# Row maxima turned by VectorE, DMAs and ScalarE instead of a TensorE transpose, for five of eight row tiles

## The chip, the cores and the metric

The kernel runs on one core of a Trainium2 chip. The metric is the device time of one execution, in microseconds; of the kernel before, three runs gave a median of 757.19 us (756.47 to 757.96). All arithmetic is 32-bit floating point.

## The reference

For each of 8 samples of 1024 rows by 256 columns an adaptive layer norm, an attention and a feed-forward stage follow each other. Cut to what matters:

```python
h = _layernorm(x) * (1 + ca) + sa
scores = einsum('nsd,ntd->nst', h * w_lhs, h * w_rhs)
x = x + ga * einsum('nst,ntd->nsd', softmax(scores, axis=2), h)
h = _layernorm(x) * (1 + cb) + sb
x = x + gb * (relu(h @ W1 + b1) @ W2 + b2)
```

The softmax takes the maximum of each row of scores away before the exponential. This maximum is what the change is about.

## The kernel before, in words

A sample b has 8 row tiles i of 128 rows. The scores are symmetric up to the two weight vectors that are folded in, so `direct` (L403) computes only the blocks on and right of the diagonal on TensorE; ScalarE copies them out of PSUM (L419), and `mirror` (L424) fills in the blocks left of it: VectorE turns 32x32 blocks (L435), four DMAs write them to a scratch tensor in DRAM (D_m, L306), and one DMA reads them back into the score tile sc (L309).

Three helpers then make the weights of a tile.

- `row_max` (L461): VectorE reduces the tile's 1024 scores to m, one maximum for each of 128 rows, one in each partition (L463).
- `max_turn` (L466): TensorE multiplies m, repeated along the columns, with the identity in transpose mode. The result pm in PSUM holds the 128 maxima along a row, the same row in every partition (L468).
- `subtract` (L471) and `exponent` (L483): VectorE subtracts pm from the eight blocks of scores into pT (L475), ScalarE takes the exponential in place (L484).

The products with pT run on TensorE as `product` (L493) or, for the pairs of tiles (1,2), (3,4) and (6,7) from the second sample on, in `pair_begin` and `pair_end` with seven products of halves in place of eight; GpSimd makes the sums of the halves (L565, L575 to L577).

The order of the work is written out by hand, in the loop over b and i that begins at L1150, and `pin` keeps every engine to it. Tile (b, i) is processed together with the scores of the tile two further on (`ahead`, L1153); its maxima are taken in the iteration before the one that turns them. In iteration i of sample b the feed-forward stage of sample b-1 (its second layer's sums, Y) runs in between:

- `pair_products` (L728) issues five or six feed-forward products for a block c and, between two of them, calls the function that it was handed, which is `max_turn` in iterations 0, 1 and 4. ScalarE's copy `kept` (L747) comes before that call.
- in iterations 2, 3, 6 and 7 `max_turn` is called inside `y_first`, `y_second` or `pair_begin`.
- the second sample is special at its start: in (1, 0) the maxima of two tiles are turned, those of (1,0) in the first `pair_products` and those of (1,1) in the second one (L1243), and only then comes the exponential of (1,0) (L1245).

The feed-forward stage's results go through DRAM as well to be turned: `turn_blocks` and `y_turn` (L316, L862) on VectorE, four DMAs out (D_a, D_f, D_y, L306), one back (X_a, X_f, Y, L309). All of these DMAs are issued by SyncE (SP) in one order; the read waits at SP for its four writes to land. X_a feeds ScalarE's rT and lT (L342), which the next sample's scores use; X_f feeds hT (L705, L707) and GpSimd's sums hs (L714 to L717), which `pair_products` uses; Y is added to x by GpSimd (L880).

PSUM is held in three pools: two buffers for scores, two for transposes and pm, and four (`ps_a`) for all other products, so a product waits until VectorE has read the one that had its buffer.

Of the kernel before, what the change touches and what calls it, by code (L numbers as in the profile page):

```python
# [11 lines left out]
F32 = mybir.dt.float32  # L12
# [5 lines left out]
P = 128  # L18
# [6 lines left out]
def adaln_block_kernel(  # L25
# [13 lines left out]
    nc = tc.nc  # L39
    B, S, D = x.shape  # L40
# [5 lines left out]
    TH = HALF // P  # L46
    H2 = HALF // 2
    NH = NI // 2
    V = 32
    NV = P // V  # L50
    DX = D + 4

    const = ctx.enter_context(tc.tile_pool(name="const", bufs=1))
    two = ctx.enter_context(tc.tile_pool(name="two", bufs=2))
    work = ctx.enter_context(tc.tile_pool(name="work", bufs=3))
# [38 lines left out]
    early_d = two.tile([P, 4, D], F32, tag="X", name="early_d", bufs=1)  # L94
# [7 lines left out]
    def load_x0(q, queue):  # L102
# [11 lines left out]
        out=wv[ND : 2 * ND, :], in_=w_rhs.rearrange("a b (k p) -> (a b k) p", p=P)  # L114
# [19 lines left out]
    ident = const.tile([P, P], F32, name="ident")  # L134
# [5 lines left out]
    def warm(n):  # L140
# [9 lines left out]
            name=nc.get_next_instruction_name(),  # L150
# [6 lines left out]
    NC_ = ND * B  # L157
# [1 line left out]
        nc.tensor.transpose(pt_c[:, ts(k, B)], c_sb[:, ts(k, P)], ident[:B, :B])  # L159
    scT = const.tile([P, ND, B], F32, name="scT")  # L160
    scf = scT.rearrange("p k b -> p (k b)")
    den = const.tile([P, NC_], F32, name="den")
    nc.scalar.activation(den, pt_c[:, :NC_], AF.Exp, scale=-1.0)

    def silu():
# [90 lines left out]
    def prepare_start(b):  # L256
        xg_t[b] = two.tile([P, NT, DX], F32, tag="xg", name=f"xg_{b}")
        nc.gpsimd.memset(xg_t[b][:, :, D : D + 1], 1.0)
# [134 lines left out]
    def score_row(b, i):  # L393
        if b == 0:
            return first_scores()[:, i].rearrange("p (n v) -> p n v", v=V)
        return sc_t[b].rearrange("p i a j v -> p j (i a) v")[:, i]
# [61 lines left out]

    max_t, pT_t = {}, {}

    def row_max(b, i):  # L461
        m = work.tile([P, 1], F32, tag="m", name=f"m_{b}_{i}")
        nc.vector.tensor_reduce(m, score_row(b, i), AX.XY, ALU.max)  # L463
        max_t[b, i] = m

    def max_turn(b, i):  # L466
        pm = ps_t.tile([P, HALF], F32, tag="t", name=f"pm_{b}_{i}")
        nc.tensor.transpose(pm[:, :P], max_t.pop((b, i)).to_broadcast([P, P]), ident)  # L468
        pT_t[b, i] = pm

    def subtract(b, i):  # L471
# [48 lines left out]


    XS = D - P + 1
    tsum = const.tile([P, 4, TH, P + 4], F32, name="tsum")
    nc.gpsimd.memset(tsum[:, 1, :, P : P + 1], 1.0)

    def right_sums(b, which):

        xg = xg_t[b]
        b11, b12 = xg[:, 0:TH, P:D], xg[:, 0:TH, 0:P]
        b21, b22 = xg[:, TH:NT, P:D], xg[:, TH:NT, 0:P]  # L530
        t = [tsum[:, n, :, 0:P] for n in range(4)]
        ins = [(b12, b11), (b22, t[0]), (b22, b12), (t[1], b21)]
        for n in which:
            nc.gpsimd.tensor_tensor(t[n], *ins[n], ALU.subtract)
# [44 lines left out]
    def pair_end(b, i):  # L579

        (s2, s4), (s3, a22) = halves(pT_t.pop((b, i))), halves(pT_t.pop((b, i + 1)))
        s1 = two_t.pop("s1")
        pq = ps_a.tile([P, HALF], F32, tag="a", name=f"pq_{b}_{i}")
        pr = ps_a.tile([P, HALF], F32, tag="a", name=f"pr_{b}_{i}")
        for out, lhs, rhs in (
            (pr[:, P : 2 * P], s1, tsum[:, 0, :, 0:P]),
            (pq[:, XS : XS + P], a22, tsum[:, 3, :, 0:P]),
            (pr[:, 2 * P : 3 * P], s3, tsum[:, 2, :, 0:P]),
            (pq[:, 0:XS], s2, tsum[:, 1, :, 0:XS]),
            (pr[:, 0:P], s4, xg_t[b][:, TH:NT, 0:P]),  # L590
        ):
            for t in range(TH):
                nc.tensor.matmul(  # L593
                    out, lhsT=lhs[:, t, :], rhs=rhs[:, t, :],
                    start=(t == 0), stop=(t == TH - 1),
                )
        two_t[b, i] = two_t[b, i][0], pq, pr
# [411 lines left out]
    def first_rows():  # L1009

        pr = ps_a.tile([P, HALF], F32, tag="a", name="prow")
        nc.tensor.matmul(
            pr[:, :HALF],
            lhsT=ident[:, 0:1].to_broadcast([P, P]),
            rhs=early_c[:, 0:2, :].rearrange("b j d -> b (j d)"),
            start=True,
            stop=True,
        )
        return pr
# [7 lines left out]
    def make_gcol():  # L1027
# [9 lines left out]
    pr = first_rows()  # L1037
# [6 lines left out]
        ALU.mult,  # L1044
    )
    row_max(0, 0)
    xg_half(0)
    mirror(0, 0)
    xg_half(1)
    keep_rows(pr, 1)  # L1050
    direct(0, 2)
    max_turn(0, 0)
    row_max(0, 1)
    for g in range(2):
        x_plus(0, g)
    subtract(0, 0)
    mirror(0, 1)
    exponent(0, 0)
    mod_rows(3, 2)
    max_turn(0, 1)  # L1060
    subtract(0, 1)
    while queue:
# [87 lines left out]
    for b in range(B):  # L1150
        for i in range(NT):
# [8 lines left out]
            if (b, i) == (0, NT - 2):  # L1160

                prepare_turn(1, 1)
                product(b, i)
                direct(*ahead)
                exponent(*last_exponent)
                product_out(b, i)
                mirror(*ahead)
                early(b, i)
                for _ in range(4):
                    spare()  # L1170
                norms(b, i)
                row_max(*ahead)
                late, last_exponent = ahead, None
                continue
            if ahead and ahead != (0, 2):
                direct(*ahead)
            if b == 0:
# [17 lines left out]
                if ahead[0] == 0:  # L1195
                    max_turn(*ahead)
# [8 lines left out]
                if i == NT - 1:  # L1205
                    assert not queue
                    right_sums(1, range(4))
# [80 lines left out]
            else:  # L1288
# [5 lines left out]
                if i == 2:  # L1294
                    left_sums(b, 1)
                elif i == 3:
                    pair_begin(b, i, turn_max)
                elif i == 6:
                    pair_begin(b, i, lambda: (max_turn(*late), weights(*late)))
                elif not ahead:  # L1300

                    pair_end(b, i - 1)
                    pair_out(b, i - 1)
                    pair_stats(b, i - 1)
# [48 lines left out]
            if i in (0, 5):  # L1353
                product(b, i)
                product_out(b, i)
            elif i == 1:
                pair_begin(b, i)
                pair_begin_sum(b, i)
            elif i == 3:
                left_sums(b, i)  # L1360
            elif i in (2, 4) or i == NT - 1 and ahead:
                pair_end(b, i - 1)
                pair_out(b, i - 1)
                if i == NT - 1:
                    assert not queue
                    right_sums(b + 1, range(4))
                if i == NT - 1 or b == B - 1:
                    pair_stats(b, i - 1)
# [8 lines left out]
    b = B - 1  # L1377
# [74 lines left out]
```

## Time and profile before

| What | Value |
|---|---|
| median of three runs | 757.19 us |
| the profiled execution's own time | 756.93 us |
| its span, first to last instruction | 755.1 us |
| PE idle, all waits of its matmuls together | 2.7 us |
| mean granted clock of TensorE | 1.000 |
| DMA packets, of these under 512 B | 106213, 29700 |
| exponentials, subtractions, maxima, turns of maxima | 64 each |

The profile is of one execution on the one core. PE is TensorE's matmul, PEld its weight load, DVE VectorE, ACT ScalarE, POOL GpSimd, SP SyncE; SPq marks a DMA issue by SP. Busy times of engines overlap. A line of the timeline gives the start, the length, the engine, the source line, the operation and its tiles, and in brackets how long the engine was idle before it and what ended that. A sample takes about 90.5 us, and from the third sample on the pattern repeats with that period.

### The profile page before, as it was taken

Reading aid. Unit: us, or ns where it says so; the run is one execution under the profiler, and the core shown is the slowest. Engines: PE = TensorE matmul, PEld = TensorE weight load, DVE = VectorE, ACT = ScalarE, POOL = GpSimd, SP = SyncE. Lnnn points to the kernel's source line nnn. Section 1 sums busy time; section 2 is a strip of 40 time slices with the busy share of each in tenths; the row PEclk is TensorE's granted clock in tenths of the full one; section 3 lists DMA queues with packets and bytes.
Section 4 is the critical chain, followed back from the end, with each engine's and each line's share of the span. In section 5 each row is a group of like instructions: output and inputs, shape, how many; then the busy total and the mean of one; then the engine's idle time right before and its main releaser. Section 6 shows DMA issues by size and latency. Waiting matters only on the chain.

```text
span 755.1 us, 11883 instructions
## 1 busy us (share of the span) xinstructions
PE 749.1 (99%) x3876; PEld 623.4 (83%) x3876; DVE 574.9 (76%) x1259; ACT 374.9 (50%) x688; POOL 570.9 (76%) x658
## 2 busy tenths in 40 slices
PE   8999999999999999999999999999999999999998
PEld 4686889788897888888888878988889788888887
DVE  7787879778796879968878688876889777685632
ACT  4554646635375454745546444563546535252521
POOL 3762796878968798788877699777996888669741
PEclk9999999999999999999999999999999999999999
DMA  9033442455443453445534555245553354133220
GB/s 308 16 112 98 131 133 74 135 178 152 127 120 123 153 153 110 147 118 158 164 99 119 153 154 161 74 127 172 155 152 85 119 166 133 50 91 126 84 85 28
DMA packets 106213, 95.21 MB, mean 126 GB/s; under 512 B 29700, under 2 KB 98848, under 8 KB 106152
## 3 DMA queue, kind: packets, MB, share of 16 engines
q1 hardware_dynamic: 98408, 85.81, 38.6%
q10 hardware_dynamic: 7744, 8.65, 3.7%
q8 instruction: 30, 0.49, 0.3%
q14 instruction: 31, 0.25, 0.1%
HBM read 50.62 MB, written 43.81 MB: 125 GB/s over the span
## 4 chain that ended last, share of the span: by engine, by line
PE 96%; DMA 1%; DVE 1%; ACT 1%; issue 0%
PE psc L412 16%; PE pa L726 11%; PE po L501 10%; PE pr L593 7%; PE pb L726 7%; PE pc L726 7%; PE yc L806 6%; PE ya L806 6%; PE yb L806 6%; PE pq L593 5%; PE pp L549 5%; PE py L916 4%; PE yd L806 3%; DMA wm<-in_L_wmod_dram 1%; PE pm L468 1%; PE pmr L194 0%
## 5 line engine op out<-in xcount | busy, mean ns | idle before, releaser
L412 PE MATMUL psc<-rT,lT 128*128 128x512 f32 (+3 forms) x384 | 134.8, 487 | 0.0
L780 POOL TENSOR_TENSOR f<-f,kept 128x512 f32<-128x512 f32 x64 | 81.5, 1274 | 42.8 <-DVE f L779 20.1
L419 ACT COPY sc<-psc 128x512 f32<-128x512 f32 (+3 forms) x96 | 44.7, 476 | 119.9 <-PE psc L412 113.0
L484 ACT ACTIVATE pT<-pT 128x1024 f32<-128x1024 f32 x64 | 67.6, 1056 | 70.6 <-DVE pT L475 70.5
L475 DVE TENSOR_TENSOR pT<-sc,pm 128x1024 f32<-128x1024 f32 x64 | 77.3, 1208 | 29.3 <-PE pm L468 13.7
L412 PEld LDWEIGHTS psc<-rT,lT 128*128 128x128 f32 x384 | 66.4, 191 | 37.2 <-issue 25.6
L501 PE MATMUL po<-xg,pT 128*128 128x257 f32 x352 | 80.6, 380 | 0.0
L463 DVE TENSOR_REDUCE m<-sc 128x1 f32<-128x1024 f32 x64 | 77.4, 1209 | 2.2 <-ACT sc L419 1.8
L501 PEld LDWEIGHTS po<-xg,pT 128*128 128x128 f32 x352 | 66.2, 190 | 10.0 <-issue 0.7
L747 ACT COPY kept<-pa 128x512 f32<-128x512 f32 x64 | 37.4, 584 | 69.3 <-PE pa L726 69.1
L726 PE MATMUL pb<-hs,w1s 128*128 128x256 f32 x256 | 65.9, 380 | 0.1
L726 PE MATMUL pc<-hT,w 128*128 128x256 f32 x256 | 65.7, 379 | 0.0
L880 POOL TENSOR_TENSOR x<-x,Y 128x512 f32<-128x512 f32 x28 | 35.1, 1276 | 29.3 <-DMA Y<-D_y 29.3
L789 ACT ACTIVATE f<-f 128x512 f32<-128x512 f32 x64 | 39.8, 622 | 34.7 <-POOL f L780 34.7
L642 POOL TENSOR_TENSOR x<-x,rows 128x256 f32<-128x256 f32 x64 | 44.8, 732 | 13.8 <-ACT rows L1022 10.6
L726 PEld LDWEIGHTS pb<-hs,w1s 128*128 128x128 f32 x256 | 48.5, 190 | 7.3 <-DVE f L765 0.8
L726 PEld LDWEIGHTS pc<-hT,w 128*128 128x128 f32 x256 | 48.6, 190 | 6.7
L806 PE MATMUL yc<-f,w2s 128*128 128x256 f32 x224 | 51.3, 379 | 0.0
L435 DVE STREAM_TRANSPOSE Tm<-sc 128x896 f32<-128x896 f32 (+6 forms) x49 | 34.3, 701 | 20.3 <-ACT sc L419 19.6
L806 PEld LDWEIGHTS yc<-f,w2s 128*128 128x128 f32 x224 | 41.5, 190 | 8.1 <-issue 2.9
L549 PEld LDWEIGHTS pp<-xg,pT 128*128 128x128 f32 x336 | 41.9, 192 | 5.1 <-DVE st_b L241 1.4
L799 POOL TENSOR_TENSOR ft<-f 128x256 f32<-128x256 f32 x56 | 40.8, 729 | 6.8 <-ACT f L790 6.8
(166 smaller groups left out, 1821.1 us busy)
## 6 DMA issues: line engine op xcount, KB each, us to landing
D_f<-T_f SPq DMA_DIRECT2D x60, 128.0 KB, 2.5
X_f<-D_f SPq DMA_DIRECT2D x15, 512.0 KB, 3.7
D_a<-T_a SPq DMA_DIRECT2D x56, 128.0 KB, 2.8
D_y<-T_y SPq DMA_DIRECT2D x56, 128.0 KB, 2.9
Y<-D_y SPq DMA_DIRECT2D x14, 512.0 KB, 3.4
out_dram<-x SPq DMA_DIRECT2D x14, 512.0 KB, 4.4
X_a<-D_a SPq DMA_DIRECT2D x13, 512.0 KB, 3.4
x<-in_L_attn_x_dram ACTq DMA_DIRECT2D x12, 512.0 KB, 3.4
```

Of the source, the lines that this page charges most:

```text
L412: nc.tensor.matmul(psc[:, : hi - lo], lhsT=lT_t[b, i // TH][:, k, ts(i % TH, P)], rhs=rT_t[b, n][:, k, lo - n * HALF : HALF], start=(k == ...
L419: nc.scalar.copy(score_row(b, i)[:, lo // V : hi // V, :], psc[:, : hi - lo].rearrange("p (n v) -> p n v", v=V),)
L463: nc.vector.tensor_reduce(m, score_row(b, i), AX.XY, ALU.max)
L475: nc.vector.tensor_tensor(pT.rearrange("p j (a v) -> p j a v", v=V), score_columns(b, i), pm[:, :P].rearrange("p (j a v) -> p j a v", j=1, ...
L484: nc.scalar.activation(pT_t[b, i], pT_t[b, i], AF.Exp)
L501: nc.tensor.matmul(po[:, : D + 1], lhsT=pT[:, t, :], rhs=xg_t[b][:, t, 0 : D + 1], start=(t == 0), stop=(t == NT - 1),)
L549: nc.tensor.matmul(out, lhsT=lhs[:, t, :], rhs=xg_t[b][:, h * TH + t, P : P + XS], start=(t == 0), stop=(t == TH - 1),)
L593: nc.tensor.matmul(out, lhsT=lhs[:, t, :], rhs=rhs[:, t, :], start=(t == 0), stop=(t == TH - 1),)
L642: queue.append(lambda: nc.gpsimd.tensor_tensor(out, in0, row, op))
L726: nc.tensor.matmul(out, lhsT=lhsT, rhs=rhs, start=True, stop=True)
L780: nc.gpsimd.tensor_tensor(f[:, c::NH, hi], f[:, c::NH, hi], kept[:, None, hi].to_broadcast([P, 2, H2]), ALU.add,)
L806: nc.tensor.matmul(out, lhsT=lhs(c), rhs=rhs(c), start=(c == 0), stop=(c == NH - 1))
```

## The change

For tiles 0, 1, 2, 4 and 5 of the samples b = 1 to 7, 35 tiles in all, `max_turn` no longer uses TensorE. `row_max` itself starts the work: VectorE turns 32x32 blocks of m, repeated to 32 columns, into mb, so that the partitions 0, 32, 64 and 96 each hold 32 of the maxima in a row; four DMAs on SP's queue, one for each of these partitions, copy its 128 bytes into all 128 partitions of mt, from SBUF to SBUF; and at the place where `max_turn` stood, ScalarE copies mt into the PSUM tile pm. The subtraction reads pm as before. The other 29 turns stay on TensorE.

mb and mt have one buffer each. To make room, the rows of xg lose two unused columns (DX), two small tiles change their layout (tsum) or move into a tile that has room (den). The other engines' orders do not change.

```diff
-    DX = D + 4
+    DX = D + 2
...
-    den = const.tile([P, NC_], F32, name="den")
+    den = early_d[:, 2, P : P + NC_]
...
+    in_time = lambda b, i: b > 0 and i in (0, 1, 2, 4, 5)
+
     def row_max(b, i):
         m = work.tile([P, 1], F32, tag="m", name=f"m_{b}_{i}")
         nc.vector.tensor_reduce(m, score_row(b, i), AX.XY, ALU.max)
         max_t[b, i] = m
+        if not in_time(b, i):
+            return
+
+        mb = work.tile([P, V], F32, tag="mb", name=f"mb_{b}_{i}", bufs=1)
+        nc.vector.transpose(mb, m.to_broadcast([P, V]))
+        mt = max_t[b, i] = work.tile([P, NV, V], F32, tag="mt", name=f"mt_{b}_{i}", bufs=1)
+        for a in range(NV):
+            nc.sync.dma_start(
+                out=mt[:, a],
+                in_=mb[a * V : a * V + 1].rearrange("o (n v) -> o n v", n=1).to_broadcast([1, P, V]),
+            )
 
     def max_turn(b, i):
         pm = ps_t.tile([P, HALF], F32, tag="t", name=f"pm_{b}_{i}")
-        nc.tensor.transpose(pm[:, :P], max_t.pop((b, i)).to_broadcast([P, P]), ident)
+        m = max_t.pop((b, i))
+        if not in_time(b, i):
+            nc.tensor.transpose(pm[:, :P], m.to_broadcast([P, P]), ident)
+        else:
+            nc.scalar.copy(pm[:, :P], m.rearrange("p a v -> p (a v)"))
         pT_t[b, i] = pm
...
-    tsum = const.tile([P, 4, TH, P + 4], F32, name="tsum")
-    nc.gpsimd.memset(tsum[:, 1, :, P : P + 1], 1.0)
+    tsum = const.tile([P, 4 * TH * P + TH * 4], F32, name="tsum")
+    tsum_first = tsum[:, : TH * (P + 4)].rearrange("p (t d) -> p t d", t=TH)
+    tsum_rest = tsum[:, TH * (P + 4) :].rearrange("p (n t d) -> p n t d", n=3, t=TH)
+    tsum_of = lambda n: tsum_first if n == 1 else tsum_rest[:, n - (n > 1)]
+    nc.gpsimd.memset(tsum_first[:, :, P : P + 1], 1.0)
```

More of the change, by code (lines that the diff above doesn't have):

```diff
@@ L530, in right_sums @@
         b21, b22 = xg[:, TH:NT, P:D], xg[:, TH:NT, 0:P]
-        t = [tsum[:, n, :, 0:P] for n in range(4)]
+        t = [tsum_of(n)[:, :, 0:P] for n in range(4)]
         ins = [(b12, b11), (b22, t[0]), (b22, b12), (t[1], b21)]
@@ L585, in pair_end @@
         for out, lhs, rhs in (
[L586 to L589, printed above, removed]
+            (pr[:, P : 2 * P], s1, tsum_of(0)),
+            (pq[:, XS : XS + P], a22, tsum_of(3)),
+            (pr[:, 2 * P : 3 * P], s3, tsum_of(2)),
+            (pq[:, 0:XS], s2, tsum_of(1)[:, :, 0:XS]),
             (pr[:, 0:P], s4, xg_t[b][:, TH:NT, 0:P]),
```

## The prediction

> **What bounds the kernel now.** I read the page's busy lines first, then the waits of PE, then the PE timeline around one turn of the maxima.
>
> ```profile
> PE 749.1 (99%) x3876; PEld 623.4 (83%) x3876; DVE 574.9 (76%) x1259; ACT 374.9 (50%) x688; POOL 570.9 (76%) x658
> PE   8999999999999999999999999999999999999998
> ```
>
> PE is busy in 99% of the span and in every slice. All waits of its matmuls together are 2.7 us, nearly all in the head. So PE's work sets the end: what leaves PE is gained, unless something that PE waits for gets late.
>
> ```profile
> 99.72 0.27 PE L468 MATMUL pm<-ident,m 128*128 128x128 f32 x1
> 99.82 1.89 PE L806 MATMUL ya<-ft,w2s 128*128 128x256 f32 x8
> ```
>
> The reader is to see the starts, not the lengths: the turn is 0.27 us long, but the next matmul starts 0.10 us after it (0.11 at 77.30 and 245.07). Matmuls overlap; a turn holds PE for 0.11 us.
>
> **What goes.** 35 turns of 0.11 us: 3.8 us. All of it is on PE, whose neighbours close up. [...]
>
> **What comes, off PE.**
> - DVE, 35 small turns. The trace has 32x32 turns of 128x256 (0.433 us) and 128x128 (0.270); on that slope 128x32 takes 0.15 (estimate), and about 0.1 to wait for the reduction's result. 0.25 x 35 = 9 us, beside 180 us of idle DVE. It counts where DVE is late already.
> - ACT, 35 copies like L419's 128x128 (0.247 us): 9 us beside 50% idle. But ACT works in order: a copy whose mt has not landed holds up all that is queued behind it.
> - SP, 140 issues of 0.44 us (D_m's median 434 ns): 1.75 us for a tile, and whatever SP issues next is late by up to that.
> - The landing. No row has a copy from one partition to 128. Nearest are D_m's writes of 16 KB, 128 packets of 128 B as here: 1.5 to 1.9 us from issue.
>
> ```profile
> L306 SPq DMA_DIRECT2D D_m<-Tm x4: 431/442/454, 304.6 to 306.1; - x4
> DMA to landing us min/median/max: 1.5/1.7/1.9
> ```
>
> The last of four issues starts 1.35 us after the first, so from the first issue to the landing I take 1.35 + 1.9 = 3.2 us; bounds 2.8, and 4.6 where the DMAs stand behind a big read: D_y's writes took 2.3 us on a free queue (302.8) and 3.3 behind sc's read (252.2). [...]
>
> - Layouts (DX, tsum, den): nothing either way. Matmuls from tsum (row step 132) and from xg (260) both take 275 ns in L593, GpSimd's sums of 128x512 1.27 us from every layout.
>
> **Where lateness reaches PE.** I laid the five copies into sample 3, then looked for the samples with the least slack.
>
> Tiles 2 and 4: SP is idle when m is ready (265.5, 286.6), mt lands at about 269.0 and 290.1, ACT gets to the copy at 269.1 and 290.6. Free.
>
> Tile 5: sc's read issues until 297.7, mt lands at about 300.9, but ACT is there at 299.4, ahead of Y's gates (L857). These start 1.7 us late; their turn (L867, 301.48) has 1.3 us of slack against them. About 0.1 us here, in samples 1, 4, 5 and 7 nothing, as sc's read was earlier.
>
> Tile 1, samples 2 to 7: the copy ends before or up to 1 us after ACT's `kept`, and ACT then idles before its next one (1.47 us at 259.88). Y is late by about 1.6 us; GpSimd's add of Y has 1.0 to 2.1 us between Y's landing and its start, and idles up to 1.5 us soon after. Taken as 0.
>
> Tile 1, **sample 1**, is different: ACT has the copy of (1,1) ahead of the exponential of (1,0), and PE wants that exponential at once.
>
> ```profile
> 78.90 0.59 ACT L747 COPY kept<-pa 128x512 f32<-128x512 f32 x1 [2.12 <-PE pa L726]
> ...
> 79.66 1.06 ACT L484 ACTIVATE pT<-pT 128x1024 f32<-128x1024 f32 x1 [0.17 <-DVE pT L475]
> ...
> 80.43 0.27 PE L468 MATMUL pm<-ident,m 128*128 128x128 f32 x1
> ...
> 80.81 1.44 PEld L501 LDWEIGHTS po<-xg,pT 128*128 128x128 f32 x7
> ```
>
> The exponential ends at 80.72, the product's first load is at 80.81: no slack. SP:
>
> ```profile
> 70.26 0.61 SPq L309 DMA_DIRECT2D sc<-D_m  x1
> 70.92 2.09 SPq L306 DMA_DIRECT2D D_m<-Tm  x4
> 75.39 0.52 SPq L309 DMA_DIRECT2D sc<-D_m  x1
> ```
>
> (1,0)'s four mt issues come between the first two lines: D_m starts at 72.7, its last write at 74.3, and lands (2.1 us) at 76.4; the read goes from 75.39 to 76.4. Then mt's last issue starts at 78.3 and lands at 80.3 (bounds 79.8 and 81.6). Copy to 80.55, exponential to 81.6, product at 81.85 where PE, two turns lighter, wants it at 80.75: a stall of **1.1 us** (0.6 to 2.4).
>
> Tile 0, **sample 6**: sc's read is 2 us later there than in sample 3, and VectorE is already late.
>
> ```profile
> 526.72 0.19 PEld L726 LDWEIGHTS pa<-hT,w 128*128 128x128 f32 x1 [0.24 <-DVE rl L614]
> ```
>
> Reciprocal L614 ended at 526.42: 0.3 us of slack. The subtraction (518.62) waited for sc, read at 514.74. mt behind it lands at about 518.7, copy to 518.95: 0.4 us late, with the small turn after the next L463 0.65, and PE comes 0.11 earlier: 0.65 + 0.11 - 0.3 = **0.45 us** (0 to 1.2). Elsewhere 0.67 us of slack and 1.4 us of DVE waiting for PE cover it.
>
> The scores of (7,0) already waited for rT (590.88, a load 0.6 us late): PE coming earlier and tile 5 of sample 6 (Y's gates 1.3 us late): **0.2 us** (0 to 0.5).
>
> **The sum**, against the profiled execution's own 756.93 us (span 755.1 and 1.8 around it; 0.26 below the median of 757.19): 3.8 gained, 1.1 + 0.45 + 0.2 + 0.1 = 1.9 given back, so 756.93 - 1.9 = **755.0 us**. 0.2%, about what a measurement of this kernel can tell from no change, is 1.5 us, so the bound is at 755.4.
>
> **Rivals.**
> 1. *All of it arrives*: 756.93 - 3.8 = 753.1. For it: D_m's landings of 1.5 us, and that sample 6's late read comes from one slow run of issues (507.81, 4.0 us for four against 1.8). Against: in sample 1 mt must land by 79.4, which needs an undelayed read as well.
> 2. *Most is given back*: mt lands half a us later (2.4 rather than 1.9). Sample 1 costs 1.6, sample 6 1.0, rT 0.5, tile 5 about 0.5 in samples 2, 3 and 6 together: 3.6, so 756.7.
> 3. *Slower: mt lands over a us later than I take it*, behind sc's read or because 128 packets leave one partition. From about 0.55 us more on the kernel is slower than before (rival 2 is 0.2 us on the other side); at 1 us more: sample 1 2.1, sample 6 1.5, tile 5 in samples 2, 3 and 6 through `ps_a` and rT 2.0, tile 1's held-up `kept` in four samples 0.25 each: 6.6 against 3.8, so 759.7. For it: 3.3 us of D_y behind sc. Against: 16 KB are an eighth of D_y's.
> 4. *It doesn't do what it says*: the 0.11 us were not PE's own, for instance since the load after a turn sets the pace. 756.9. Against: eight matmuls before a turn take 8 x 0.216 up to the turn's very start.
>
> **How the numbers follow.** Forecast 0.33 (own range 754.2 to 755.8; 0.27 of it faster by over 0.2%, 0.06 within). Rival 1: 0.20, faster. Rival 2: 0.27 (0.24 within, 0.03 slower). Rival 3: 0.17, slower. Rival 4: 0.03, within. Faster 0.47, same 0.33, slower 0.20. The range runs from rival 1 with its last tenth, 753.0, to rival 3's 759.7.
>
> **What would show it.** PE's matmuls of pm fall from 64 to 29 and PE's busy time by some 4 us; PE's waits rise from 2.7 to about 4.6, the largest at the first product of (1,0), released by L484, then at pa of sample 6, released by VectorE. mt's landings should be 1.5 to 1.9 us on a free queue. Wrong if landings are above 2.5, if ACT's copies wait for mt in most tiles 0 and 1, or if waits stand at products that I called covered.

## The result and the profile after

The changed kernel takes **793.51 us** (median; 792.0 to 798.22), the kernel before took 757.03 in the same series (756.47 to 757.96): a ratio of 1.049 (95% interval 1.045 to 1.054), 36.5 us slower. The forecast was 755.0 with a range up to 759.7. The profiled execution has a span of 791.6 us at a mean granted clock of 0.989 (before: 755.1 at 1.000).

The page's busy line and PE's slices, after:

```profile
PE 758.9 (96%) x3841; PEld 624.9 (79%) x3841; DVE 582.1 (74%) x1294; ACT 383.2 (48%) x723; POOL 567.3 (72%) x658
...
PE   8999899999979999899899998999998999999998
```

35 matmuls are gone, and yet PE's busy time has grown by 9.8 us and its idle time (span less busy) from 6.0 to 32.7. The waits of its matmuls (total, times, longest) say for whom:

```profile
PE pa L749 <- ACT kept L770: 23.6, 11, 4.1
PE po L521 <- ACT pT L504: 2.9, 1, 2.9
```

Both are results of ScalarE. What ScalarE waited for shows in the view of the tile mt (issues, copies, waits, landing):

```profile
L476 SPq DMA_DIRECT2D mt<-mb x140: 498/600/1235, 70.9 to 696.8; - x140
L488 ACT COPY pm<-mt x35: 269/269/277, 76.2 to 699.5; 128x128 f32<-128x128 f32 x35
...
  DMA mt<-mb: 73.3, 31
...
DMA to landing us min/median/max: 2.5/2.7/3.8
```

The reader is to see four numbers: an issue takes 0.60 us, a landing 2.7 us, and 31 of the 35 copies stood and waited, 73.3 us together. From the first of the four issues to the copy the waiting ones took 4.57 to 6.01 us, median 4.67.

The turns that are left on TensorE are as they were:

```profile
L486 PE MATMUL pm<-ident,m x29: 271/272/322, 24.4 to 718.4; 128*128 128x128 f32 x29
```

The largest single wait of the forecast, at the product of (1,0), is where it was expected, but larger. The same stretch of the timeline as in the prediction:

```profile
70.88 2.55 SPq L476 DMA_DIRECT2D mt<-mb  x4
...
77.82 2.44 SPq L476 DMA_DIRECT2D mt<-mb  x4
...
82.42 0.27 ACT L488 COPY pm<-mt 128x128 f32<-128x128 f32 x1 [3.11 <-DMA mt<-mb]
...
82.62 1.05 ACT L504 ACTIVATE pT<-pT 128x1024 f32<-128x1024 f32 x1
...
83.73 0.48 PE L521 MATMUL po<-xg,pT 128*128 128x257 f32 x1 [2.88 <-ACT pT L504]
```

ScalarE stands 3.11 us at the copy of (1,1), and the exponential of (1,0), which PE needs, is queued behind it.

The largest group of waits is new. Tile 5 of sample 3, after:

```profile
298.95 2.43 SPq L476 DMA_DIRECT2D mt<-mb  x4
...
301.73 1.75 SPq L306 DMA_DIRECT2D D_a<-T_a  x4
...
305.97 1.80 SPq L306 DMA_DIRECT2D D_m<-Tm  x4
...
310.33 0.59 ACT L770 COPY kept<-pa 128x512 f32<-128x512 f32 x1 [0.49 <-PE pa L749]
...
311.00 0.55 SPq L309 DMA_DIRECT2D sc<-D_m  x1
...
311.65 2.50 SPq L476 DMA_DIRECT2D mt<-mb  x4
...
316.27 0.27 ACT L488 COPY pm<-mt 128x128 f32<-128x128 f32 x1 [5.35 <-DMA mt<-mb]
...
318.32 0.57 ACT L770 COPY kept<-pa 128x512 f32<-128x512 f32 x1
...
318.94 1.22 PE L749 MATMUL pa<-hT,w1s 128*128 128x256 f32 x2 [3.90 <-ACT kept L770]
```

The first mt is tile 4's. Tile 5's mt has to wait at SyncE behind the read of scores (311.00), so its issues start at 311.65; ScalarE, ready at 310.92, stands 5.35 us; then come Y's gates, two small activations and `kept`, and PE has waited 3.90 us.

After some of these waits PE does not run at its full clock for a while. Windows of six microseconds over the same place (length, PE's busy time and matmuls, granted clock, DMA share, GB/s):

```profile
306.00:312.00 6.00, 6.00 (x29) 1.00 0.40 113
312.00:318.00 6.00, 3.04 (x15) 0.97 0.16 33
318.00:324.00 6.00, 5.06 (x21) 0.50 0.39 98
324.00:330.00 6.00, 6.00 (x41) 0.96 0.61 186
```

**Where the 36.5 us of span come from.** Idle time of PE: 32.7 - 6.0 = 26.7. Clock: in windows of 1 us, one stretch of 3.4 us at half clock follows each of the waits that end at 221.67, 416.49 and 477.88; at 318.94 it is 6.8 us, from 317.6 on, of which PE still stood for 1.3. PE worked 15.8 us at half clock and lost half of that, 7.9: two products of 128x256 take 0.85 us there, start to start (478.79), and 0.43 at full clock (228.75). The turns: -3.3 (PE's busy time falls by that much in e2b_no_dma below). That leaves about 5.2. The loads of pa and po wait 31.9 us for ScalarE where their matmuls are shown to wait 26.5. If in these 5.4 us the last matmul before a wait counts as busy and does no work, they are the rest; that is an estimate from the two numbers, and no run shows it by itself.

### The profile page after: what moved, and what is told of

Same layout as the page of the kernel before. It is cut to its first block, busy times and chain, and to the rows that moved or that the text cites. A ratio compares the mean times of both kernels' runs of the same rounds, so it can differ in the third digit from the quotient of the medians.

```text
span 791.6 us, 12221 instructions
## 1 busy us (share of the span) xinstructions
PE 758.9 (96%) x3841; PEld 624.9 (79%) x3841; DVE 582.1 (74%) x1294; ACT 383.2 (48%) x723; POOL 567.3 (72%) x658
## 4 chain that ended last, share of the span: by engine, by line
PE 51%; DMA 14%; POOL 9%; DVE 8%; SPq 8%; issue 6%; ACT 4%; DVEq 0%; ACTq 0%; POOLq 0%
PE psc L412 8%; PE po L521 7%; DMA D_m<-Tm 5%; PE pa L749 5%; DMA mt<-mb 5%; PE pr L616 4%; SPq L306 4%; PE py L939 3%; PE ya L829 3%; PE yb L829 3%; PE pb L749 3%; PE pq L616 3%; SPq L476 3%; POOL tsum L557 3%; PE pc L749 3%
## 5 line engine op out<-in xcount | busy, mean ns | idle before, releaser
L495 DVE TENSOR_TENSOR pT<-sc,pm 128x1024 f32<-128x1024 f32 x64 | 77.3, 1208 | 47.1 <-DMA sc<-D_m 24.2
L412 PEld LDWEIGHTS psc<-rT,lT 128*128 128x128 f32 x384 | 66.3, 190 | 37.7 <-issue 24.2
L749 PE MATMUL pa<-hT,w1s 128*128 128x256 f32 x128 | 40.7, 403 | 23.6 <-ACT kept L770 23.6
L737 POOL TENSOR_TENSOR hs<-hT 128x256 f32<-128x256 f32 x16 | 11.6, 728 | 64.3 <-DVE hT L728 64.3
```

Of the source, the lines that this page charges most:

```text
L412: nc.tensor.matmul(psc[:, : hi - lo], lhsT=lT_t[b, i // TH][:, k, ts(i % TH, P)], rhs=rT_t[b, n][:, k, lo - n * HALF : HALF], start=(k == ...
L495: nc.vector.tensor_tensor(pT.rearrange("p j (a v) -> p j a v", v=V), score_columns(b, i), pm[:, :P].rearrange("p (j a v) -> p j a v", j=1, ...
L749: nc.tensor.matmul(out, lhsT=lhsT, rhs=rhs, start=True, stop=True)
```

## The experiments

Theory A, from the trace above: ScalarE's copy waits in order for an mt that lands too late. Theory B: the 140 issues hold up what SyncE issues after them, whoever reads mt. Every kernel was timed beside the kernel before on the same chip; "+4.8" is the median less that of before (757.2 to 758.1).

**e1_dma_unused: the DMAs alone.**

```diff
-        mt = max_t[b, i] = work.tile(...)
+        mt = work.tile(...)
...
-        if not in_time(b, i):
             nc.tensor.transpose(pm[:, :P], m.to_broadcast([P, P]), ident)
-        else:
-            nc.scalar.copy(pm[:, :P], ...)
```

> The small turns and the four DMAs of the changed kernel stay, but nobody reads mt: TensorE makes all 64 turns of the maxima as before. Theory A (ScalarE's copy waits for mt, and kept behind it makes PE wait): 757 to 760 us, PE's waits near 3 us. Rival B (140 more issues on SP's queue make sc, X_f and Y late, and PE waits for those): 780 us or more, with the same waits as after. The slots of the four issues themselves should stay at about 0.6 us and the landings at 2.5 to 2.7 us either way.

769.92 us, +11.9, ratio 1.015 (1.013 to 1.017). Neither theory gave this number: B's share is there, but a third of the whole. PE's waits in it:

```profile
PE pa L746 <- ACT kept L767: 9.5, 5, 2.8
```

All five are in iteration 1 of a sample. In sample 3: mt of tile 0 is issued from 243.69 to 246.19, D_f starts right after it at 246.23, and X_f is read at 251.62 (before 246.73, with PE 1 us earlier); then mt of tile 1, and Y is read at 264.02 (before 257.00). GpSimd's sum with Y waits for that read, the sum that ScalarE's relu needs stands behind it on GpSimd, `kept` stands behind the relu, and PE waits for `kept`.

**e3_no_copy: VectorE's subtraction reads mt in place, no copy.**

```diff
+        if in_time(b, i):
+            pT_t[b, i] = m.rearrange("p a v -> p (a v)")
+            return
         pm = ps_t.tile(...)
```

> VectorE's subtraction reads mt from SBUF, ScalarE's copy is gone; the DMAs stay. The wait for mt moves from ScalarE's place to VectorE's, which comes 0.3 to 6 us later. A: most of the 36 us come back, 754 to 762 us, and the waits of PE for kept are gone. B: 785 us or more. In between (765 to 780) both have a share.

772.76 us, +14.7, ratio 1.020 (1.018 to 1.021). With all 35 turns off TensorE and all DMAs, 22 of the 36.5 us are gone when ScalarE does not stand at mt. So both theories have a share. The waits for `kept` that are left (7.1 us in five, and one of 1.4 put down to VectorE) are all in iteration 1, none at tile 5.

**e4_copy_late: the copy moved to the subtraction.**

```diff
     def subtract(b, i):
         pm = pT_t.pop((b, i))
+        if in_time(b, i):
+            m, pm = pm, ps_t.tile(...)
+            nc.scalar.copy(pm[:, :P], m.rearrange("p a v -> p (a v)"))
```

> ScalarE's copy stays, but stands where the subtraction is issued rather than where the transpose stood, so for tile 5 the gates of Y and kept come before it; for tiles 1 and 2 kept of the next block still comes after it. A: 757 to 770 us, waits for kept left only at tiles 1 and 2. B: 785 us or more.

793.02 us, ratio 1.047 (1.042 to 1.051): no gain, and a miss. The copies' waits for mt fell to 30.9 us, but tile 5's copy now stands behind ScalarE's rT and lT (L342, 3 us), the subtraction waits for it, and PE waits 2.34 us for VectorE in each of six samples. The stall was moved, so this run does not judge A.

**e2b_no_dma: small turns and copies, no DMAs.**

```diff
-        mt = max_t[b, i] = work.tile(...)
-        for a in range(NV):
-            nc.sync.dma_start(...)
+        max_t[b, i] = still
```

> Without the 140 DMAs: VectorE's small turns and ScalarE's copies stay, the copies read a constant tile that is ready from the start, 29 turns are left on TensorE (the maxima taken away are wrong, 20 in place of each row's). Theory (both losses, SyncE's queue and ScalarE's waiting copies, come from the DMAs alone): the whole gain shows, 753.0 to 754.5 us, and PE's waits stay at 3 us or less. Rival (the added turns and copies themselves, or the changed layouts, cost time): 756 us or more.

753.60 us, -4.1, ratio 0.995 (0.993 to 0.996). The whole gain of the prediction is there (3.8 were worked out). PE's busy line, to be held against 749.1 and 755.1:

```profile
span 752.3 us, 11885 instructions
...
PE 745.8 (99%) x3841; PEld 620.2 (82%) x3841; DVE 580.5 (77%) x1294; ACT 380.7 (51%) x723; POOL 568.3 (76%) x659
```

The copies read a constant here, so the maxima are not used; but the added work is all there. So VectorE's turns, ScalarE's copies and the layouts cost nothing that shows; all of the loss comes through the DMAs.

**e5_own_partition: e1 with another source.**

```diff
-                in_=mb[a * V : a * V + 1].rearrange(...).to_broadcast([1, P, V]),
+                in_=mb,
```

> As e1_dma_unused (mt is written by four DMAs and read by nobody, TensorE makes all 64 turns), but each DMA copies the 128 partitions of mb to the same partitions of mt: the same 128 packets of 128 bytes, not all from one partition. Theory 'one partition is slow': an issue goes from 601 ns to about 440, the landing from 2.7 to at most 2.0 us, and the time from 769.9 to 758 to 763. Rival 'any such DMA from SBUF to SBUF takes this long': issue 560 to 620 ns, landing 2.5 to 2.8 us, 767 to 772.

771.33 us, +13.6, ratio 1.018 (1.016 to 1.020), issue 0.601 us, landing 1.8/2.4/4.2 us (min/median/max; e1 had 2.5/2.7/3.9). The rival holds, its landing but for 0.1 us: that all packets leave one partition is not what makes the issue long, and of the landing it is 0.3 us in the median.

**e12_two_issues and e13_one_issue: would the prediction have held with its own landing?**

```diff
-        for a in range(NV):
+        for a in range(2):    # e13: range(1)
             nc.sync.dma_start(out=mt[:, a], ...)
```

> As changed, but only two of the four DMAs are issued (the other 64 maxima of a row are a constant 20): SyncE is held 1.25 us a tile in place of 2.5, and from first issue to landing it takes about 0.6 + 2.7 = 3.3 us, near the 3.2 of the prediction. Theory 'a size was off, not a step': with the landing as sized the prediction's sum comes out, 753.5 to 757 us, PE's waits at most 6 us. Rival 'tiles 0, 1 and 5 can't take it at 3.3 us either': 762 us or more.

> As before with one DMA of four (96 maxima constant): SyncE is held 0.6 us a tile, first issue to landing about 2.7 us. Both theories: 753 to 755.5 us, nearly all of the 4 us. If it is above 757, a wait for one round trip of a DMA is too long by itself, however few the issues.

Two issues: 770.65 us, +13.2, ratio 1.017 (1.013 to 1.022). From the first issue to the copy the waiting ones took 3.3 us at least, 3.7 in the median, where the prediction has 3.2 to the landing. Half a us more is what its second rival prices, at 1.7 us. One issue: 758.76 us, +1.3, ratio 1.001 (1.000 to 1.003), a miss of both theories; landings 2.3/2.5/4.5 us, and 13 copies still waited, with a median of 3.1 us from the issue. PE stood 1.91 us for `kept` at tile 5 of sample 3 and 0.77 us at (1,0). The theory "a size was off, not a step" fell: two DMAs cost 13 us where the prediction's sum has a gain of 1.9, and even one, about as fast as the prediction took the four, eats up the gain. In e12 (here the tile that is read is called `still`):

```profile
  DMA still<-mb: 35.8, 22
...
DMA to landing us min/median/max: 2.5/3.0/4.4
```

22 of 35 copies still wait.

**Tile by tile.** These kernels differ from the changed one in one line, here that of e6. (The waits that the expectations place "at pa of iteration 5" stand, by the loop's index, in iteration 4, the one that turns tile 5.)

```diff
-    in_time = lambda b, i: b > 0 and i in (0, 1, 2, 4, 5)
+    in_time = lambda b, i: b > 0 and i in (0, 1, 2, 4)
```

> Tile 5 is turned by TensorE again, tiles 0, 1, 2 and 4 as changed. Theory 'ScalarE's copy of tile 5 is the largest part': the 13.7 us of PE's waits in its iteration and the lower clock with them go, 0.7 us of gain goes too: 775 to 781 us. Rival 'the waits stand there only because lateness from tiles 0 to 4 comes out there': 787 us or more, and waits at pa of iteration 5 stay at 2 us or more in samples 2 to 6.

> Only tiles 2 and 4 are changed, 14 turns off TensorE. If they are free, as the prediction took them: 758.0 - 14 x 0.11 = 756.0 to 757.0 us. If the lateness of SyncE's queue or ScalarE's wait reaches PE from these two as well: 759 to 766 us, with waits at pa, released by kept, in the second half of each sample.

> Only tile 5 is changed, 7 turns (0.8 us) off TensorE. Theory 'the parts add to more than their sum': without tile 4's four issues ahead of them on SyncE, tile 5's start 2.4 us earlier, the copy waits about 3 us in place of 5.4, and of that 1.5 to 1.8 us are slack: PE waits for kept 1 to 1.5 us in the three samples with the late read (2, 3, 6), with no drop of the clock: 757.7 - 0.8 + 4 = 759 to 763 us. Rival 'tile 5's copy is by itself the 26 us by which the changed kernel is longer than the one without tile 5': 772 us or more, waits of 3 us or more.

> Tiles 4 and 5 are changed, 14 turns (1.5 us) off TensorE; tile 4 by itself was free beside tile 2. Theory 'tile 4's issues make tile 5 late': waits at pa, released by kept, of 3 to 4 us in samples 2, 3 and 6 as in the changed kernel, 10 to 14 us together, and 3 to 9 us by the clock that halves after them: 768 to 780 us. Rival (the two don't touch each other): tile 5's time less 0.8 us.

> Only tile 0 is changed, 7 turns off TensorE. Its four issues put D_f and X_f 2.5 us later or more on SyncE. Theory 'the slack behind X_f takes most of it': waits of at most 1 us a sample, 756 to 760 us. Rival 'tile 0 is what makes kept of iteration 1 late': 762 us or more.

> Only tile 1 is changed, 7 turns off TensorE. Its issues put D_y and with it Y behind, on which the sum of Y, the relu and kept of iteration 1 depend. Theory 'tile 1 by itself gives about half of the 12 us of tiles 0 and 1': 759 to 764 us, with waits of 0.5 to 1.2 us at pa of iteration 1. Rival 'only both together use up the slack': 756 to 758 us, no such waits.

> Tiles 0 and 1 are changed, 14 turns off TensorE. Alone they cost 4.0 and 3.0 us. Theory 'lateness adds up within a sample: each tile's issues delay SyncE's next read of scores, from which the next maxima come': 766 to 771 us, as tiles 2 and 4 are no longer free behind them. Rival (it's the sum): 764 to 766 us.

> Tiles 2, 4 and 5 are changed, 21 turns (2.3 us) off TensorE. Theory 'the 26 us that tile 5 adds to tiles 0, 1, 2 and 4 come only when the sample is late already from tiles 0 and 1': 762 to 767 us. Rival 'tiles 2, 4 and 5 make most of it by themselves': 774 us or more, with waits at pa of iteration 5 of 3 us or more.

| Tiles changed | Median, us | Against before | Ratio, 95% interval |
|---|---|---|---|
| 2, 4 (e7) | 755.76 | -1.9 | 0.997 to 0.999 |
| 5 (e8) | 762.65 | +4.8 | 1.005 to 1.008 |
| 0 (e10) | 761.78 | +4.0 | 1.004 to 1.007 |
| 1 (e11) | 760.84 | +3.0 | 1.002 to 1.006 |
| 0, 1 (e14) | 769.52 | +12.1 | 1.013 to 1.019 |
| 4, 5 (e9) | 765.26 | +7.4 | 1.008 to 1.014 |
| 2, 4, 5 (e15) | 770.70 | +13.2 | 1.015 to 1.022 |
| 0, 1, 2, 4 (e6) | 767.56 | +9.9 | 1.012 to 1.016 |
| all five | 793.51 | +36.5 | 1.045 to 1.054 |

Three things follow. Tiles 2 and 4 are free by themselves, and no cost of theirs shows behind tiles 0 and 1 (e6 is 2 us below e14, about their gain, though the intervals overlap). The prices do not add: one by one 4.8 + 4.0 + 3.0 - 1.9 = 9.9, together 36.5. And what does not add is mostly tile 5, which costs 4.8 alone, 15 behind tiles 2 and 4 (e15 less e7) and 27 behind all the others (all five less e6); tiles 0 and 1 add 5 more together.

e8, e11 and e14 came out in the first range of their expectation, but e14's reason, that tiles 2 and 4 would no longer be free, is not borne out by e6. e10 lies between its two ranges, with four waits of 0.5 to 1.5 us; e7 is 0.2 us better than its first. e6 fell below both of its ranges. e9 lies between its two: the waits did not come in its trace (1.7, 0.9 and 1.1 us, not 3 to 4), which is of the fastest of four runs (762.3; two others took 767 and 768). e15 lies between its two, with waits from 1.4 to 4.2.

Why tile 5 costs more behind others is seen where it is alone, in the same sample 3 of e8:

```profile
298.40 0.53 SPq L309 DMA_DIRECT2D sc<-D_m  x1
...
298.98 2.56 SPq L476 DMA_DIRECT2D mt<-mb  x4
...
300.62 0.59 ACT L770 COPY kept<-pa 128x512 f32<-128x512 f32 x1 [0.49 <-PE pa L749]
...
303.66 0.27 ACT L488 COPY pm<-mt 128x128 f32<-128x128 f32 x1 [2.46 <-DMA mt<-mb]
...
305.71 0.57 ACT L770 COPY kept<-pa 128x512 f32<-128x512 f32 x1
...
306.33 0.70 PE L749 MATMUL pa<-hT,w1s 128*128 128x256 f32 x2 [1.01 <-ACT kept L770]
```

The copy waits 2.46 us and PE 1.01: 1.45 of slack. With all five tiles it was 5.35 and 3.90: again 1.45. So every microsecond beyond the slack reaches PE whole. The difference of 2.9 us is SyncE's read of scores: here it starts 2.2 us ahead of `kept`, with all five tiles 0.7 us behind it. That read waits for the D_m writes ahead of it.

What puts it back in this sample is not the mt that SyncE issues just before: D_a, behind tile 4's mt, starts at 301.73, when VectorE has just written T_a (until 301.70), and the mt issues had ended at 301.38; in e9, where tile 4's mt stands in the same place, the read is 2.3 us ahead of `kept`, about as in e8. In e15, which changes tile 2 as well, it is 0.8 us behind, as with all five. First e9, then e15:

```profile
298.63 0.55 SPq L309 DMA_DIRECT2D sc<-D_m  x1
...
300.93 0.59 ACT L770 COPY kept<-pa 128x512 f32<-128x512 f32 x1 [0.49 <-PE pa L749]
...
306.54 0.70 PE L749 MATMUL pa<-hT,w1s 128*128 128x256 f32 x2 [0.90 <-ACT kept L770]
```

```profile
301.34 0.59 ACT L770 COPY kept<-pa 128x512 f32<-128x512 f32 x1 [0.49 <-PE pa L749]
...
302.13 0.55 SPq L309 DMA_DIRECT2D sc<-D_m  x1
...
310.30 1.01 PE L749 MATMUL pa<-hT,w1s 128*128 128x256 f32 x2 [4.24 <-ACT kept L770]
```

Of the 3.1 us between the two, 1.9 are there when the last D_m writes are issued. Tile 2's mt stands ahead of them, and so does a read of X_f (249.94) that took 5.7 us to land where e9's took 3.8 at most. The rest is the landing of these writes, 3.8 to 4.4 us against 2.8 in e9 (3.9 in the median with all five tiles, 2.1 in the kernel before). How much is tile 2's mt in itself, and why DMAs land later here, is not shown.

**e16_pool_queue: mt's DMAs off SyncE.**

```diff
-            nc.sync.dma_start(out=mt[:, a], ...)
+            nc.gpsimd.dma_start(out=mt[:, a], ...)
```

> As changed, all five tiles, but mt's DMAs are issued by GpSimd on its own queue, so that SyncE issues what it did before the change; GpSimd now waits in order for mb and spends time on each issue, which no trace here prices. Theory 'SyncE's order carries the lateness from tile to tile': SyncE's reads of scores are on time again (VectorE's waits for sc back near the 11 us of before, from 24 us), ScalarE waits less than half of 73 us for mt, and the time is under 780 us, unless GpSimd's sums come late. Rival 'ScalarE's waits by themselves are enough': ScalarE still waits 60 us or more for mt, 785 us or more.

799.35 us, +42.2, ratio 1.057 (1.055 to 1.058): slower still. The reads of scores are on time again (VectorE waits 6.9 us for sc; 24.2 in the changed kernel), but GpSimd, which issues in order too, now waits itself:

```profile
POOL mt L476 <- DVE Y L871: 29.3, 7, 4.8
POOL mt L476 <- DVE mb L473: 16.5, 1, 16.5
```

mt comes late from there as well (ScalarE waits 69.4 us for it), and GpSimd's sums hold up PE. The theory's numbers did not come and the rival's did, but with this new wait the run cannot tell the two apart. How much of the growth from tile to tile is carried by SyncE's order and how much by ScalarE's waits **stays open**.

**e17_2_4_no_copy and e18_no_5_no_copy: reading in place with fewer tiles** (e3's edit and e7's or e6's).

> Only tiles 2 and 4 are changed, and VectorE's subtraction reads mt where it is, without ScalarE's copy. Tiles 2 and 4 with the copy gave 755.76 us against 757.69, all waits of PE being those of the head. Theory 'ScalarE's copies cost nothing there': the same again, 755.5 to 756.2 us. Rival 'the copies' own waits for mt (11 us) still cost something': below 755.3 us.

> Tiles 0, 1, 2 and 4 are changed, tile 5 is turned by TensorE, and VectorE reads mt in place, without ScalarE's copies. With the copies this was 767.6 us; all five tiles without copies 772.8, with them 793.5. Theory 'ScalarE's waiting copies cost PE only at tile 5 and in sample 1, the rest is SyncE's lateness': 763 to 768 us, the 2.8 us of (1,0) gone, 1 to 2 us a sample at pa of iteration 1 left. Rival 'the copies of tiles 0, 1, 2 and 4 cost as much as that of tile 5': below 760 us.

e17: 756.18 us, -1.0, ratio 0.999 (0.998 to 0.9995), not better than with the copy; the copies of tiles 2 and 4 cost nothing. e18: 772.41 us, +14.4, ratio 1.018 (1.017 to 1.020): a miss on both sides, 4.5 us *slower* than with the copies (+9.9). Without the copies VectorE stands at mt in place of ScalarE (12.5 us in 6 waits), and its subtraction takes longer: 1.47 us in the mean where it reads mt in SBUF, 1.21 where it reads pm, which is 7 us more for 28 tiles. Which of the two costs the 4.5 us was not tried.

Tile 5 adds 0.3 us where all maxima are read in place (e3 against e18) and 26.6 where all go through ScalarE's copy. The read of scores is late without the copies too: in sample 3 of e3 it starts only 0.3 us ahead of `kept`, and yet no matmul waits there. So the 22 us that e3 won over the changed kernel come from ScalarE's copy of tile 5 behind late tiles, not from the copies as such. A kernel with the copies of tiles 0, 1, 2 and 4 and only tile 5 read in place was not run.

The best version is e7, tiles 2 and 4 alone: 0.24% faster than before (interval 0.15 to 0.33%).

## Why the prediction was wrong, point by point

- **The gain: right.** 35 turns at the distance of their starts, 0.11 us, were worked out as 3.8 us; without DMAs the kernel gained 4.1. The turns' length, 0.27, would have promised 9.6 (64 of them took 0.274 us in the mean before, L468).
- **VectorE's turn and ScalarE's copy hidden: right.** 0.21 and 0.27 us each (taken as 0.15 and 0.247), and free in e2b. For the wait on the reduction's result, taken as 0.1 us, the trace after has 0.03 to 0.04 from its end to the start of the small turn (34 of 35).
- **SyncE's issue: 0.44 taken, 0.60 measured**, so four take 2.5 us, not 1.75.
- **First issue to landing: 3.2 us taken, 4.6 measured**, at the upper end of the bounds 2.8 to 4.6. The rows of D_m's writes (1.5 to 1.9) were too short for a copy inside SBUF (2.5 to 3.8), and the end that the prediction kept for "behind a big read" is what it takes on a quiet queue (4.7 in e7 at 265.47, where SyncE had issued nothing for 1.6 us; 4.6 in the changed kernel at 298.95, after 2.2 us without an issue).
- **(1,0) of sample 1: the place and the cause right, the size not.** 1.1 us (0.6 to 2.4) were forecast, 2.88 measured. With tile 1 alone (e11) it is 1.10, which is chance: that run leaves out tile 0, which the sum has, and its mt lands 1.5 us later than the sum takes.
- **"Tiles 2 and 4 ... Free": right by themselves** (e7), wrong in that tile 5 costs 15 us behind them and 4.8 alone (e15, e8).
- **"Tile 1, samples 2 to 7 ... Taken as 0": wrong.** Tile 1 alone costs 3.0 us and its gain of 0.8. In the trace 1.10 us of that are sample 1; 1.4 and 1.6 are waits for `kept` in two later samples.
- **Tile 0 "0.45 us": wrong.** Tile 0 alone gives four waits of 0.5 to 1.5 us and +4.0 us.
- **Tile 5 "about 0.1 us": wrong, and the largest term.** The prediction looked at the turn of Y (1.3 us of slack). PE was reached by the other thing behind Y's gates, the second `kept`, with 1.45 of slack; alone the copy waits 2.46 there, with the others 5.35. With the 1.7 us of lateness that the prediction took, this slack would have held all but 0.25: what it had wrong was the lateness, more than the slack.
- **The step that failed.** The prediction "laid the five copies into sample 3" of the old schedule and summed slack tile by tile. e12 shows that this step is wrong even when the landing is about as it took it: +13.2 us and not -1.9. In sample 3 the trace shows what it left out: behind the earlier tiles' DMAs SyncE reads the scores 2.9 us later against ScalarE's work, so the next mt starts later still, and the slack that the prediction gave tile 5 is spent before its copy's turn comes. Of the 38.4 us between the forecast (-1.9) and the result (+36.5), 11.8 are single prices (9.9 where it had -1.9, with a landing 1.4 us longer than it took), 26.6 are that they do not add. How much of these SyncE's order carries and how much ScalarE's waits is open (e16); that ScalarE's copy is needed for them is shown (e3, e18).
- **The third rival** had the side and the reason right ("mt lands over a us later"). All three signs of being wrong came: landings above 2.5, copies waiting in most tiles 0 and 1, waits at products called covered. Its price of 759.7 was made by the same tile-by-tile sum and so was too small: it has 0.25 us in four samples for tile 1's `kept`, where waits for `kept` in iteration 1 came to 9.9 us in six samples, and tile 5 in a part of 2.0 us, where PE waited 13.7 in five.
- **The clock** was not in the prediction at all; it is 7.9 of the 36.5 us.

## What to carry to other kernels

A DMA round trip (4.7 us here, from the first issue to the copy) put in the place of a tenth of a microsecond on the bounding engine has to be laid into the schedule as it will be, with the earlier round trips already late in it; where the same queue also brings the data from which the next round trip is made, single slacks must not be added (here 9.9 us one by one, 36.5 together). Count for an in-order engine everything that stands behind the waiting instruction, and follow all of it to the bounding engine, not only the nearest consumer. Try the tiles one by one: two of five were worth keeping here.

## What the runs showed of the hardware

- **Half clock after a wait.** After some waits of PE in the changed kernel the granted clock was 0.50 for 3.4 us or, once, 6.8 (from 317.6 on); each 3.4 us in which PE worked at it lost 1.7, on top of the wait. It followed a wait of 1.92 us (416.49) but not one of 3.38 us (609.21: clock 1.00 up to 621). What decides which waits it follows is not shown.
- **Issues on SyncE differed by kind.** 0.60 us for one copy of 16 KB inside SBUF, with one or with 128 source partitions (the changed kernel and e5), against 0.44 for D_m's writes of 16 KB to DRAM (before, 304.6 to 306.1). GpSimd issued the same copies in 0.53 us (e16), with landings of 2.8 us in the median (2.7 from SyncE) and about the same time from the first issue to the copy (4.6 us in the median of those that waited).
- **The subtraction took longer with the maxima in SBUF.** VectorE's 128x1024 subtraction took 1.21 us with the maxima in PSUM (pm) and 1.34 to 1.47 us in the mean with mt in SBUF (e17, e3, e18).
- **Waits of PE cost more than idle time.** In the changed kernel they show in the idle time (26.7 us), in the clock after some of them (7.9) and, by the estimate above, in busy time that is no work (about 5); the idle time alone would have explained three quarters of the loss of 36.5.
